# Orders from a scheduler that plays queues and transfers in time, on the bounded path of a two-layer block

## The chip, the cores and the metric

The kernel runs on one core of a Trainium2 chip. Its engines are TensorE (PE, with its weight loads listed apart as PEld), VectorE (DVE), ScalarE (ACT), GpSimd (POOL) and SyncE (SP, which here issues transfers). Each engine works through its own instructions in a fixed order; semaphores hold an instruction back until what it needs from another engine or a transfer is there. The metric is the device time of one launch in microseconds (us). Beside it stands one execution recorded by the hardware profiler; times within it are counted from the start of its span.

## The reference

Two pre-norm layers over 8 sequences of 256 tokens with 256 features, all in fp32. Every block is `x = x + f(layernorm(x))`.

```python
# layer 0, attention: 16 heads of 16; one projection, normed three times
w = x @ W.T;  q, k, v = rms_norm(w, g1), rms_norm(w, g2), rms_norm(w, g3)
att = q @ k.T / 4
y = (softmax(att, -1) + softmax(att, -2)) @ v;   return y @ W
# layer 0, experts: 4 experts, the best 2 of each token, hidden 512, and a shared one of 256
y = sum(combine[:, e] * ((silu(x @ w1[e].T) * (x @ w3[e].T)) @ w2[e].T))
y = y + (silu(x @ sw1.T) * (x @ sw3.T)) @ sw2.T
# layer 1, RWKV-4 time mixing: token shift, three projections, a recurrence over time
xk, xv, xr = (x * tm + shift(x) * (1 - tm) for tm in (tm_k, tm_v, tm_r))
k, v, r = xk @ Wk.T, xv @ Wv.T, sigmoid(xr @ Wr.T)
rwkv = r * layernorm(wkv(decay, first, k, v)) * ln_g + ...;   return rwkv @ Wo.T
# layer 1, experts: 8 experts, the best 2, hidden 256, with biases
h = x @ w1[e].T + b1[e];  y = glu * sigmoid(1.702 * glu) * (lin + 1);  ye = y @ w2[e].T + b2[e]
```

## The kernel before

**Two paths.** A bound on the attention scores is worked out on the device from the gains. With the inputs used it holds, so the first branch of an If is taken: `layers(True)`, the bounded path. It contains everything after the first sequence's norm.

**Units of work.** The sequences form two groups, 0 to 4 and 5 to 7. For each layer and group there is an `Experts` object: `one` and `two` in layer 0 (22 and 15 tiles of 128 gathered tokens are run), `three` and `four` in layer 1 (24 and 16). When all of a group's sequences have their logits (L784), `choose` picks the best two experts of each token, `route` works out which rows go to which tile (L704 to L866, two matmuls at L823 and L824), and `fill` builds the rows' numbers (`here`, `goes`, L885 to L922, matmul L906). Each takes many small DVE operations.

**An expert tile** is: a gather `xg` by POOL (L996); two transposes on PE (L1006) and a copy by ACT (L1008); on PE's sequencer a read of the tile's expert number (`whose`, L1021), by which the weights are addressed; up products (L1014, with w1s and w3s in layer 0, v1s in layer 1); silu on ACT (L1033 or L1028) and a product on DVE (L1035; in layer 1 L1026 and L1029); transposes and a copy again; the down product (L1014, w2s or v2s); out of PSUM by ACT (L1043) or DVE (L1041); a scatter `back` by POOL (L1044). `tiles` overlaps three tiles: it issues the gather of j+3, the transposes of j+1, the up product of j and the down product of j−2 together. After the regular tiles come `spare_tiles`, which read a count (L958) and branch past tiles that are not needed (L962); none of the spare ones runs with these inputs. The shared expert of layer 0 is `shared`: two up products, silu (L944), a product (L945), a down product (L950) and an add to x (L953). `combine` loads the rows back (`y`, L1097 on SP), adds them to x on DVE (L1105, four per sequence), and in layer 1 stores the output (L1109).

**Time mixing** goes through ten stages per sequence. Each step of the generator runs a different stage for each sequence that is under way, so that sequences overlap by a fixed lag:
- norm: statistics (L210, L211) on DVE, a power on POOL (L216, L217), `nb` (L203), `xr` on ACT (L235)
- mix: transposes on PE (L246), a copy on ACT (L1145), `dx` and six `mix` operations on DVE (L1135, L1153)
- project: the matmuls for k, v and r (L1164); k and v are copied by ACT (L1172), r goes through tanh (L1170)
- exponents: scan `pp`, `ex` and `d` on DVE (L1180, L1135); six relus (L1190 to L1192) and two Exps (L1194) on ACT
- denominator, invert, numerator: on DVE a scan `bb` (L1203), `den`, the reciprocal (L1211), a scan `aa` (L1218), `num`
- norm_inner: transposes (L1230) on PE, statistics `st` and `mv` on DVE (L1235, L1236), POOL's power, `z` on ACT (L1241)
- gate, project_out: transposes of z (L246), `num` on ACT (L1251), a product on DVE (L1254), matmuls (L1261), the add to x (L1135)

After them the sequence is normed for the experts (`xm` on ACT, L235), stored for the gathers (L768), transposed (`xmT`), and its logits are computed (L779, L784).

**What sets the order.** The program is written in an order of its own, by `weave`, which draws from several generators in fixed proportions; a tile scheduler then places the instructions on the engines by priority, which is that order but for `tc.high_priority` (an offset of 60 for the stages of time mixing, 3000 for the routing) and `tc.issue_after`, which keeps one instruction behind another. PE's order in the attention part is under `tc.manual_schedule`, that is, as written. The stretch with the most streams is this:

```python
weave((back, 4), (take(mixing, 3), 3), (take(tiles, 5), 5))      # one's combine, two's tiles
weave((take(mixing, 24), 24), (behind(tiles), 13))               # two's tiles
back = two.combine(yp)
...
with tc.issue_after(three.routed.ins):
    weave((shared, 4))                                           # two's last shared products
ctx0.close()                                                     # layer 0's weights end here
...
weave((take(behind(tiles, 3), 20), 20), (mixing, 15))            # three's tiles, sequences 5 to 7
```

`behind(tiles, lag)` keeps each step of the tiles behind a matmul that a sequence has issued. Layer 1's weights (24 transfers by SP, L1308 to L1340) lie where those of layer 0 were, so they wait for the last shared product.

Of the kernel before, what the change touches and what calls it, by code (L numbers as in the profile page):

```python
# [70 lines left out]
def two_layers(  # L71
# [1401 lines left out]
        turned_in = {0: turned(xn, lnp, "xmT1", lambda shape: p0.tile(shape, F32, tag="ps", name="ps"), nc.scalar, bufs=2)}  # L1473
    is_flat = nc.values_load(flat[0:1, 0:1], min_val=0, max_val=1)
    with tc.If(is_flat > 0) as which:
        layers(True)
    with which.Else():
        attention_any()
        layers(False)
# [61 lines left out]
```

## Time and profile before

| | before |
|---|---|
| time, median of 2 runs (759.67 to 761.9) | 760.78 us |
| time of the profiled execution | 762.06 us |
| its span | 760.3 us |
| mean granted TensorE clock | 0.930 |
| busy: PE, DVE, ACT, POOL | 656.0, 462.6, 359.2, 244.9 us |
| moved by DMA | 66.85 MB, 88 GB/s |

By stage, in us from the start of the span, with the busy time of each engine:

| stretch | what runs | PE | DVE | ACT | POOL |
|---|---|---|---|---|---|
| 0–200 | attention, `one`'s logits | 172.2 | 154.8 | 124.3 | 66.4 |
| 200–355 | `one`'s tiles, shared expert | 152.5 | 31.4 | 45.4 | 41.4 |
| 355–530 | `two`'s tiles, sequences 0 to 4 in layer 1 | 152.7 | 119.3 | 99.6 | 45.2 |
| 530–580 | `three`'s routing, last shared products, weights | 32.3 | 44.3 | 17.5 | 10.3 |
| 580–690 | `three`'s tiles, sequences 5 to 7 | 101.6 | 80.1 | 57.6 | 56.8 |
| 690–745 | `four`'s tiles, `three`'s combine | 44.7 | 28.0 | 14.8 | 24.9 |
| 745–760 | `four`'s combine | 0 | 4.8 | 0 | 0 |

The page's parts are read so: busy time per engine; the span in forty slices with a digit of busy tenths each; groups of instructions with what ended the idle time ahead of them. In the lists of waits a row has the waiting engine, tile and line, then what released it, then the total wait, how often, and the longest. In a timeline a row has start and length in us, engine, line, operation, output and input, and in brackets the idle time ahead of it and what ended it.

### The profile page before, as it was taken

The page shows a single profiled execution, that of the slowest core. Times are in us where ns is not written, and L with a number is a line of the kernel's source. Part 1 is how long each engine was busy: PE and PEld are TensorE (multiplying, and loading weights), DVE is VectorE, ACT ScalarE, POOL GpSimd, SP SyncE. Part 2 cuts the span into 40 slices and gives each one's busy share as a digit, 9 for nine tenths or more (in the row PEclk, how much of TensorE's full clock was granted, in tenths as well). Part 3 has the DMA queues.
Part 4 walks back from the last instruction along what each step waited for, and adds up shares of the span by engine and source line. Part 5 has one row for each costly group of instructions (what it writes and reads, how often), then busy time and mean ns, then how long its engine had stood idle before and what let it go on. Part 6 is the DMA issues. An engine that isn't in the chain of part 4 may idle for free. (4 is left out here: it accounts for less than half of the span.)

```text
span 760.3 us, 10764 instructions
## 1 busy us (share of the span) xinstructions
PE 656.0 (86%) x3170; PEld 417.1 (55%) x3170; DVE 462.6 (61%) x1216; ACT 359.2 (47%) x761; POOL 244.9 (32%) x319
## 2 busy tenths in 40 slices
PE   3799999997889999998899888986838989998790
PEld 2355555545775666665466656654625756564460
DVE  6698878787361111110766887673988986755542
ACT  3687767663312333332286477544246474532230
POOL 3434333300202333333222231212040456456440
PEclk9699999988899999999999999998868999999995
DMA  7800000000301111111400110002077336568734
GB/s 205 312 1 15 15 15 15 15 15 18 94 12 31 42 43 49 37 40 52 158 29 13 42 28 22 28 28 71 29 226 257 113 118 190 157 201 259 261 125 137
DMA packets 38547, 66.85 MB, mean 88 GB/s; under 512 B 6006, under 2 KB 20654, under 8 KB 38480
## 3 DMA queue, kind: packets, MB, share of 16 engines
q1 hardware_dynamic: 30400, 47.01, 18.9%
q0 software_dynamic: 7392, 18.50, 7.9%
q8 instruction: 31, 0.51, 0.3%
q10 hardware_dynamic: 688, 0.55, 0.2%
q14 instruction: 36, 0.29, 0.1%
HBM read 51.32 MB, written 16.41 MB: 89 GB/s over the span
## 5 line engine op out<-in xcount | busy, mean ns | idle before, releaser
L996 POOL DMA_INDIRECT xg<-asked,source x77 | 78.5, 1020 | 192.1 <-PE ps L1006 166.3
L1044 POOL DMA_INDIRECT back<-yg,row_i x77 | 81.0, 1051 | 110.6 <-ACT yg L1043 34.4
L1035 DVE TENSOR_TENSOR h<-h,mm 128x512 f32<-128x512 f32 x37 | 25.3, 684 | 108.1 <-PE mm L1014 108.0
L1014 PE MATMUL mm<-v1s,xgT 128*128 x160 | 79.2, 615 | 2.3 <-ACT xgT L1008 1.4
L1008 ACT COPY hT<-ps 128x256 f32<-128x256 f32 (+1 forms) x77 | 36.4, 473 | 94.5 <-PE ps L1006 94.3
L576 ACT ACTIVATE e<-sc,minus 128x512 f32<-128x512 f32 x96 | 59.9, 712 | 31.1 <-PE sc L563 31.0
L1014 PE MATMUL mm<-w1s,xgT 128*128 x148 | 72.8, 611 | 0.2 <-issue 0.2
L1014 PE MATMUL mm<-w2s,hT 128*128 x296 | 72.2, 383 | 0.0
L577 DVE TENSOR_REDUCE s<-e 128x2 f32<-128x512 f32 x96 | 60.5, 677 | 15.9 <-ACT e L576 15.7
L1014 PE MATMUL mm<-w3s,xgT 128*128 x148 | 70.1, 593 | 0.0
L563 PE MATMUL sc<-qT,kT 32*128 32x512 f32 x256 | 58.7, 725 | 2.9 <-DVE qT L544 2.2
L1014 PEld LDWEIGHTS mm<-w2s,hT 128*128 128x128 f32 x296 | 54.0, 192 | 7.2 <-issue 1.4
L515 POOL TENSOR_TENSOR rr<-rr,minus_half 128x32 f32<-128x32 f32 x7 | 38.0, 5429 | 49.8 <-DVE rr L513 49.7
L1006 PEld LDWEIGHTS ps<-ident,h 128*128 128x128 f32 x228 | 29.1, 143 | 44.7 <-issue 28.5
L1164 PE MATMUL sc<-mix,rw 128*128 128x256 f32 x192 | 47.7, 395 | 6.0 <-DVE mix L1153 6.0
L1006 PE MATMUL ps<-ident,h 128*128 128x128 f32 x228 | 39.7, 278 | 8.3 <-DVE h L1029 7.6
L216 POOL TENSOR_TENSOR rs<-mv,eps_ln 128x2 f32<-128x2 f32 x40 | 8.6, 216 | 116.8 <-DVE mv L211 74.4
L1014 PEld LDWEIGHTS mm<-w3s,xgT 128*128 128x128 f32 x148 | 27.6, 191 | 33.3 <-issue 32.6
L1164 PEld LDWEIGHTS sc<-mix,rw 128*128 128x128 f32 x192 | 37.1, 200 | 13.8 <-DVE mix L1153 7.1
L1014 PE MATMUL mm<-v2s,hT 128*128 x160 | 42.7, 386 | 0.8 <-ACT hT L1008 0.8
L1033 ACT ACTIVATE h<-mm 128x512 f32<-128x512 f32 x37 | 22.1, 598 | 42.7 <-PE mm L1014 42.7
L1014 PEld LDWEIGHTS mm<-v1s,xgT 128*128 128x128 f32 x160 | 28.4, 197 | 23.4 <-issue 19.7
(246 smaller groups left out, 1255.9 us busy)
## 6 DMA issues: line engine op xcount, KB each, us to landing
bias<-bd SPq DMA_DIRECT2D x40, 384.0 KB, 4.0
y<-back SPq DMA_DIRECT2D x16, 512.0 KB, 4.7
asked<-xm SPq DMA_DIRECT2D x16, 256.0 KB, 2.2
x<-in_x_dram SPq DMA_DIRECT2D x8, 256.0 KB, 6.1
w1s<-in_w_dram SPq DMA_DIRECT2D x4, 512.0 KB, 9.5
w3s<-in_w_dram SPq DMA_DIRECT2D x4, 512.0 KB, 10.3
w2s<-in_w_dram SPq DMA_DIRECT2D x4, 512.0 KB, 10.2
v1s<-in_v1g_dram SPq DMA_DIRECT2D x8, 256.0 KB, 6.2
```

Of the source, the lines that this page charges most:

```text
L515: on_pool["last"] = nc.gpsimd.tensor_tensor(rr, rr, half, ALU.pow)
L563: nc.tensor.matmul(pa, lhsT=q["kT"][rows, u, ts(t, P)], rhs=q["qT"][rows, u], start=True, stop=True)
L576: nc.scalar.activation(e, pa, AF.Exp, bias=minus)
L577: nc.vector.tensor_reduce(q["s"][:, t, h : h + 2], e, AX.X, ALU.add)
L996: nc.gpsimd.indirect_dma_start(out=xgs[j], out_offset=None, in_=self.asked, in_offset=bass.IndirectOffsetOnAxis(ap=self.source[:, j : j + ...
L1006: nc.tensor.transpose(pt[:, c, :], src[:, ts(c, P)], ident)
L1008: nc.scalar.copy(to, pt)
L1014: nc.tensor.matmul(po.unsqueeze(1), lhsT=lhsT[:, c, :], rhs=w[:, ds(e, 1), c, :], start=(c == 0), stop=(c == n - 1))
L1033: nc.scalar.activation(s, pu, AF.Silu)
L1035: nc.vector.tensor_tensor(s, s, pg, ALU.mult)
L1044: inst = nc.gpsimd.indirect_dma_start(out=self.back, out_offset=bass.IndirectOffsetOnAxis(ap=self.row[:, j : j + 1], axis=0), in_=yg, in_o ...
L1164: last = nc.tensor.matmul(po[:, o, :], lhsT=w[:, c, ts(o, P)], rhs=m[:, c, :], start=(c == 0), stop=(c == NC - 1))
```

## The change

The call of the bounded path is placed in a block whose orders come from another scheduler, one that plays the program in time, with a model of queues and transfers, to choose what each engine gets next. The source of the computation is the same, and so are the written order that it starts from, the priorities, `issue_after` and the hand-written PE order of attention. The other path keeps the plain scheduler.

```diff
     is_flat = nc.values_load(flat[0:1, 0:1], min_val=0, max_val=1)
     with tc.If(is_flat > 0) as which:
-        layers(True)
+        with tc.block(schedule_with_timeline_sim=True):
+            layers(True)
     with which.Else():
         attention_any()
         layers(False)
```

In the compiled program each engine gains one unconditional branch, at the block's start. The other instructions are the same, but for reads of registers and semaphore operations that follow the new neighbours, and for ACT's table loads, of which there are 18 in place of 22 in the block after the first L962. Line numbers after 1475 are one higher.

What moves, by engine, with "#k" for the k-th of its kind:
- PE: attention as before. In the block after the first L962, `z` #k, L1261 #k, the transposes of xr #k+2 and xm #k and L1164 #k+2 stand together, with tile products ahead of them rather than between. Reads of expert numbers (L1021) stand in rows of several: four ahead of the first L950, eight ahead of the L906 of `three`, sixteen ahead of `four`'s first v1s products.
- DVE: `st` #k (L1235) stands behind `bb`, `k`, `den`, `v`, `aa` and `num` of sequence k+1, its `mv`, `nb` and L1254 behind that sequence's reciprocal (L1211). Adds of `combine` (L1105) stand among the operations of `choose`. At the start the conversions of vec and b2s (L1320, L1325) stand ahead of the first `xn`.
- ACT: z, xr, num (L1251) and xm of a sequence stand in a row, behind tile copies that were after them.
- POOL: scatters of `three`'s tiles up to 22 stand ahead of `four`'s first four gathers, which had been ahead of them.
- SP: `combine`'s loads stand earlier, several in a row.

## The prediction

> **What bounds the kernel now.** First I read the page's busy times and its forty slices of 19 us.
>
> ```profile
> PE 656.0 (86%) x3170; PEld 417.1 (55%) x3170; DVE 462.6 (61%) x1216; ACT 359.2 (47%) x761; POOL 244.9 (32%) x319
> ...
> PE   3799999997889999998899888986838989998790
> ...
> DVE  6698878787361111110766887673988986755542
> ```
>
> PE leads at 86%, so the sum of its work sets the end almost everywhere. Two stretches differ: from 360 to 530 us (two's tiles woven with the RWKV sequences 0 to 4) its digits sink to 8, and near 560 to 6, where DVE has 9. Next, what PE waited for from 357 to 530 us (total, times, longest):
>
> ```profile
> PE sc L1261 <- DVE num L1254: 6.1, 3, 2.3
> PE sc L246 <- ACT xm L235: 5.0, 5, 2.0
> PE sc L246 <- ACT xr L235: 3.5, 1, 3.5
> PE ps L1006 <- PEq L962: 2.4, 1, 2.4
> ```
>
> Nearly all are waits for a step of an RWKV sequence. With the rest they come to some 20 us; otherwise expert tiles stand between a sequence's steps in PE's order and cover its latency. Third, DVE's timeline during sequence 2 (start, duration):
>
> ```profile
> 438.30 0.76 DVE L1235 BATCH_NORM_STATS2 st<-sc 128x6 f32<-128x256 f32 x2 [0.32 <-PE sc L1230]
> ...
> 442.60 0.16 DVE L203 SCALAR_TENSOR_TENSOR nb<-mv,rs 128x2 f32<-128x2 f32 x1 [0.79 <-POOL rs L217]
> 442.68 1.27 DVE L1203 TENSOR_TENSOR_SCAN bb<-ex 128x256 f32<-128x256 f32 x2
> ...
> 445.75 0.67 DVE L1254 SCALAR_TENSOR_TENSOR num<-r,num 128x512 f32<-128x512 f32 x1
> ...
> 451.12 3.32 DVE L1211 RECIPROCAL den<-den 128x512 f32<-128x512 f32 x1
> ```
>
> The statistics and gate of sequence 1 (L1235, L1254) run before and among the recurrence of sequence 2 (bb, then the 3.3 us reciprocal). So sequence 1's output and sequence 3's start go on while sequence 2 waits for ACT's exponentials. Last, PE around the change of weights:
>
> ```profile
> 554.43 1.46 PE L950 MATMUL mm<-sw2s,hs 128*128 128x256 f32 x6
> 562.07 0.66 PE L1006 MATMUL ps<-ident,xg 128*128 128x128 f32 x2 [6.19 <-DMA xg<-asked,source]
> ...
> 570.97 7.50 PE L1164 MATMUL sc<-mix,rw 128*128 128x256 f32 x24 [3.88 <-DVE mix L1153]
> ...
> 579.33 1.10 PE L1014 MATMUL mm<-v1s,xgT 128*128 x2
> ```
>
> The weights of layer 1 take the place of layer 0's, so their loads wait for the last shared matmul (ends 555.4); the first v1s matmul comes 23.9 us later.
>
> **The change, part by part.** No arithmetic changes. Every engine gets one branch, and each keeps its instructions in another order. PE's attention order is written by hand and stays. Sums are against the profiled execution (span 760.3, time 762.1, 1.3 above the median of 760.8). "#k" is the k-th sequence.
>
> *Branch.* The page "Runtime: NRT & Kernel Launch" (section "Instruction fetch mechanics") speaks against the change: a taken branch to a target outside the current two pages must fetch it. The rows: far jumps out of the If at the end took 2.8 us (DVE 754.41 to 757.25), branches to nearby targets at L962 0.1 to 0.3 us. The new target follows directly: 0.2, ends 0.1 and 3.
>
> *Start.* On DVE the conversion of vec (its load is issued at 9.9 and lands 4.0 us later) moves ahead of the first xn (13.50), and both L217 powers go behind the second L216 on POOL. DVE waits to about 14, then follows statistics, power and xn: xn near 16.2 in place of 13.5. Some of the 2.7 is absorbed; the first score matmul comes 1.3 later (0 to 2.5).
>
> *One's tiles.* An index read (L1021) takes PE's sequencer 0.69 us to the next (178.48, 179.19, 179.87, 180.55). Four move ahead of the first shared matmul (+1.6); five leave the end of the block, where PE had 2.35 idle (−1.1): +0.5.
>
> *Two's tiles with sequences 0 to 4: the main term.* In the new order PE has z, L1261, the next xr and xm transposes and the next L1164 adjacent, with tiles ahead of the group and none inside. On DVE st#1 (L1235) stands behind bb, k, den, v, aa, h, den and num of sequence 2, so behind the wait for ACT's Exp; its mv, nb and gate L1254 stand behind the 3.3 us reciprocal too. The later sequences are alike. Behind those wait, on PE, L1261#1 and all that follows, so tiles no longer cover. One period, from the first L1164 of k to that of k+1, by the rows of the timelines:
> - k out of PSUM 2.6, pp 1.3, ex and d 1.2: 5.2
> - six relus with v and r on ACT: 9.6; table load 1.28, Exp 1.06: 12
> - bb to num on DVE, with one h: 18.7
> - st with the next st<-x 1.5, reciprocal 3.3, num and mv 0.9: 24.4
> - POOL's two powers, nb: 25.9; z on ACT, its transposes: 27.7
> - num (L1251) 1.0, L1254 0.7, L1261 1.5, with their hand-overs: 32.3
> - x+= and its statistics 1.5, dx 0.7, mix 2.9: 37.2; nb, xm and its transposes: 38.7.
>
> PE's own work in this is two tiles at 6.7 and the sequence's matmuls, about 24; 14 are idle. Before, the periods were 30.2, 25.9 and 25.2 (L1164 at 401.3, 431.5, 457.3, 482.5). In the walk #1 starts at 405.2 (nb#0 behind a combine add delays the first mix), the next period is 33.5, then 38.7, then 39.4 with a tile moved ahead: 438.7, 477.4, 516.8. The last logit of group three follows 48.4 later (46.7 before): 565.2 in place of 529.2, **+36**. If ACT and DVE catch up where I queued them strictly, +10; with a slower matmul clock in the gaps (granted 0.75 from 530 to 580, where PE was idle), +45.
>
> *Route, shared expert, weights.* choose (L704 to L812) is interleaved with a combine add L1105, whose load landed 3.2 after the logit; goes is done 3.8 later. The shared expert's last two tiles stand behind goes, pp#5 and the xr#6 transposes (at 564.9, past the last L950, before). L950 ends about 14.5 after goes, in place of 8.9; with the 3.8 that is some +10 on the start of SP's 24 weight loads and so on the first v1s: **+10.4** (5 to 15).
>
> *Three's first tiles.* L1164#7 and L1261#5 go ahead of tile 0's down product; mix#7 on DVE is ready 13 us after the first v1s: 7 idle, where 2.6 was: +4 (0 to 6).
>
> *Three to four.* On POOL the scatters of tiles up to 22 go ahead of four's first four gathers (issued 672 to 677 before, PE free at 680). A gather takes 1.0 to issue and 3.7 to land, so PE waits 4 to 6. Sixteen index reads stand in a row before four's first v1s: 11.0 us of sequencer. The trace has the sequencer at most 16 matmuls, 4 to 5 us, ahead, which leaves 6. "TensorE: Matmul & The Clock Gate" (specification table) gives PE's queue a depth of 64; with matmul and weight load as two entries that hides 7 and leaves 4. The two waits overlap: **+6** (2 to 9); by the rule it would be +5.
>
> *End.* The index reads leave four's block, but there PE was full already; two L1105 groups go ahead of h and yg: 0 ± 2. The last combine is unchanged.
>
> *ACT.* Table loads fall from 22 to 18, 5.1 us by the row's 1.28. They lie beside PE's work or inside the chain already counted: 0.
>
> **Sum:** 0.2 + 1.3 + 0.5 + 36 + 10.4 + 4 + 6 = 58.4. From 762.1 that is 820.5; less the 1.3 to the median, **819 us**.
>
> **The rivals.**
> - *Faster.* The period is shorter than I walk it: the group of RWKV steps finds its data ready since more tiles stand ahead of it. Then the 3.5 of xr, L1261's 6.1 and the branch's 2.4 go, and nothing comes back: about 749. It decides where a period stays under 25, the two tiles and the sequence's own matmuls. The 17 us of waits speak for it; st behind the reciprocal speaks against it, since no tile ahead of it on PE makes DVE earlier. 4%.
> - *No change that can be told.* PE has 656 us of work by either order, and what idles in one place is regained in the next: 762. For it: PE idles 10 us or more around 560, which could absorb a delay. Against: those waits hang on the same chain and shift with it. Here too the change that does little: attention is fixed by hand. But the block after 357 us is reordered on all five engines. 8%.
> - *Moderately slower.* The main term is only +10, for tiles cover most of the chain; with the other 22: 793, with 783 to 802 its own span. 24%.
> - *As forecast,* 802 to 846: 58%. *Slower still* (each DVE wait also delays scatters and gathers behind it on POOL, or weights come later): 850 and more, 6%.
>
> **How the numbers follow.** The range joins the forecast (its main term between +20 and +45, the small terms at their ends) with the moderate case: 783 to 846; left out are the faster case, the one without change and slower still, 18%. The bound for telling a change is about 2%, 15 us; faster takes 3% (a part of the first rival stays within the bound), within it 9%, slower 88%.
>
> **What would show it.** Right: L1164's starts near 405, 439, 477, 517; PE waiting for L1254 and xm more than 12 us per period in place of 2 to 4; L1235 just before or after the reciprocal; the first v1s near 627; PE's digits at 6 in the slices from 420 to 560; PE's busy time still near 656. Wrong: periods of 30 or less; v1s matmuls before 595; or the loss lying in attention or in four's tiles, where I give 2 and 6.

## The result

| | before | after |
|---|---|---|
| time, median of 2 runs each | 760.78 us (759.67 to 761.9) | 808.05 us (806.26 to 809.84) |
| ratio | | 1.066 (95% interval 1.060 to 1.072) |
| span of the profiled execution | 760.3 us | 808.0 us |
| granted TensorE clock | 0.930 | 0.913 |

The change makes the kernel 47 us slower; forecast were 58. From the page of after, its busy times and two rows of the forty slices (of 20.2 us each):

```profile
PE 667.0 (83%) x3170; PEld 428.8 (53%) x3170; DVE 465.9 (58%) x1216; ACT 352.8 (44%) x757; POOL 246.7 (31%) x319
...
PE   4899999996999999998997676965667799979790
...
DVE  6688787886621111108783636552878885663742
```

PE's share falls from 86% to 83%, and its row shows where: from the 22nd slice to the 30th (424 to 606 us) it has fives, sixes and sevens with a single nine, where before had mostly eights and nines up to 530 us, and DVE's digits there are 2 to 8. Neither engine is full; they wait for each other. PE's busy time rose too, by 11 us, with the same 3170 matmuls.

What PE waited for, in after, from 357 us to the last logit of group three at 561 (total, times, longest):

```profile
PE sc L246 <- ACT xm L235: 12.0, 4, 5.0
PE sc L1261 <- DVE num L1254: 11.5, 4, 6.0
PE sc L246 <- ACT z L1241: 10.5, 4, 4.4
...
PE ps L1006 <- ACTq L962: 0.7, 1, 0.7
```

The first three rows were 5.0, 6.1 and 2.1 us in before's list, whose third row is

```profile
PE sc L246 <- ACT z L1241: 2.1, 4, 0.6
```

Together they grew from 13 to 34 us. The wait at L962 has gone down from 2.4 to 0.7.

The same period of DVE as was shown of before (sequence 2's recurrence, sequence 1's statistics), now in after:

```profile
445.02 1.27 DVE L1203 TENSOR_TENSOR_SCAN bb<-ex 128x256 f32<-128x256 f32 x2 [6.25 <-ACT ex L1194]
...
451.05 0.75 DVE L1235 BATCH_NORM_STATS2 st<-sc 128x6 f32<-128x256 f32 x2
...
452.38 3.33 DVE L1211 RECIPROCAL den<-den 128x512 f32<-128x512 f32 x1
...
459.31 0.16 DVE L203 SCALAR_TENSOR_TENSOR nb<-mv,rs 128x2 f32<-128x2 f32 x1 [0.51 <-POOL rs L217]
461.90 0.69 DVE L1254 SCALAR_TENSOR_TENSOR num<-r,num 128x512 f32<-128x512 f32 x1 [2.43 <-ACT num L1251]
...
468.27 2.46 DVE L1153 SCALAR_TENSOR_TENSOR mix<-dx,vec,x 128x256 f32<-128x256 f32 x6
```

`bb` of sequence 2 starts 12.9 us after that sequence's first L1164 (432.2). The statistics of sequence 1 come behind it and `num`, their aggregation (`mv`) behind the reciprocal. L1254, which had stood at 445.75 in front of the reciprocal, ends at 462.6. PE beside it:

```profile
453.83 1.89 PE L1014 MATMUL mm<-w2s,hT 128*128 x8
459.45 1.36 PE L246 MATMUL sc<-ident,z 128*128 128x128 f32 x4 [3.73 <-ACT z L1241]
462.65 3.42 PE L1261 MATMUL sc<-rw,num 128*128 128x256 f32 x8 [1.84 <-DVE num L1254]
465.90 0.60 PE L246 MATMUL sc<-ident,xr 128*128 128x128 f32 x4
471.49 0.48 PE L246 MATMUL sc<-ident,xm 128*128 128x128 f32 x1 [4.99 <-ACT xm L235]
471.76 5.62 PE L1164 MATMUL sc<-mix,rw 128*128 128x256 f32 x16
```

After the second tile's down product PE has only z, L1261, xr and xm, one behind the other, and is idle 3.73 + 1.84 + 4.99 us between them. The tiles that covered those steps have been done earlier.

A period is the time from the L1164 of one sequence to that of the next. The windows sum the periods up; they begin some 0.3 us ahead of the first L1164 (window, its length, then busy time and instructions of PE, PEld, DVE, ACT, POOL, then PE's granted clock). Before, the whole stretch and the periods of sequences 2 and 3:

```profile
357.00:528.70 171.70, 152.10 (x634) 103.99 (x634) 118.13 (x261) 99.27 (x179) 44.07 (x57) 0.97 0.14 43
...
431.20:457.10 25.90, 23.36 (x106) 16.68 (x104) 19.66 (x43) 16.91 (x31) 7.17 (x10) 0.99 0.10 30
457.10:482.30 25.20, 21.90 (x98) 15.43 (x98) 20.38 (x47) 16.29 (x31) 5.20 (x8) 1.00 0.04 13
```

and after:

```profile
357.00:561.10 204.10, 160.01 (x634) 110.24 (x634) 118.24 (x261) 96.67 (x177) 46.01 (x58) 0.90 0.11 36
...
431.90:471.50 39.60, 27.36 (x101) 18.69 (x101) 21.08 (x47) 17.24 (x32) 7.58 (x10) 0.80 0.07 20
471.50:511.80 40.30, 33.05 (x122) 23.11 (x123) 21.71 (x48) 19.13 (x35) 5.01 (x8) 0.82 0.04 14
```

The same 634 matmuls up to the last logit take 204.1 us in place of 171.7. Of the 32.4, idle time bears 24.5 (19.6 to 44.1) and slower matmuls 7.9 (152.1 to 160.0 busy, clock 0.97 to 0.90).

The table has the shift of after against before at marks of both traces, and what each stretch adds ("tile 3" is the fourth of its group, counted from 0):

| mark | shift, us | added | forecast |
|---|---|---|---|
| first score matmul | +1.6 | +1.6 | +1.3 |
| first transposes of two's tiles | −0.6 | −2.1 | +0.7 (branch, index reads) |
| last logit of group three | +32.4 | +33.0 | +36 |
| first v1s product | +40.7 | +8.3 | +10.4 |
| v1s of three's tile 3 | +48.0 | +7.3 | +4 |
| v1s of three's tile 23, the last | +38.7 | −9.3 | 0 |
| v1s of four's tile 3 | +48.4 | +9.7 | +6 |
| v1s of four's last tile | +46.1 | −2.3 | 0 |
| end | +47.7 | +1.6 | 0 |

### The profile page after: what moved, and what is told of

It is laid out like the page before. It is cut to its first block, busy times and chain, and to the rows that moved or that the text cites. A ratio compares the mean times of both kernels' runs of the same rounds, so it can differ in the third digit from the quotient of the medians.

```text
span 808.0 us, 10830 instructions
## 1 busy us (share of the span) xinstructions
PE 667.0 (83%) x3170; PEld 428.8 (53%) x3170; DVE 465.9 (58%) x1216; ACT 352.8 (44%) x757; POOL 246.7 (31%) x319
## 5 line engine op out<-in xcount | busy, mean ns | idle before, releaser
L996 POOL DMA_INDIRECT xg<-asked,source x77 | 80.2, 1041 | 168.3 <-PE ps L1006 146.1
L1014 PE MATMUL mm<-w2s,hT 128*128 x296 | 70.0, 379 | 0.0
L563 PE MATMUL sc<-qT,kT 32*128 32x512 f32 x256 | 58.4, 693 | 3.1 <-DVE rr L513 2.4
L1164 PE MATMUL sc<-mix,rw 128*128 128x256 f32 x192 | 49.3, 412 | 1.4 <-DVE mix L1153 1.4
L1026 DVE TENSOR_TENSOR hb<-mm,bias 128x512 f32<-128x512 f32 x40 | 27.6, 689 | 34.9 <-PE mm L1014 30.1
L1164 PEld LDWEIGHTS sc<-mix,rw 128*128 128x128 f32 x192 | 39.5, 211 | 9.1 <-issue 2.4
## 6 DMA issues: line engine op xcount, KB each, us to landing
y<-back SPq DMA_DIRECT2D x16, 512.0 KB
w1s<-in_w_dram SPq DMA_DIRECT2D x4, 512.0 KB
w3s<-in_w_dram SPq DMA_DIRECT2D x4, 512.0 KB
w2s<-in_w_dram SPq DMA_DIRECT2D x4, 512.0 KB
```

Source lines behind the costliest of these rows:

```text
L563: nc.tensor.matmul(pa, lhsT=q["kT"][rows, u, ts(t, P)], rhs=q["qT"][rows, u], start=True, stop=True)
L996: nc.gpsimd.indirect_dma_start(out=xgs[j], out_offset=None, in_=self.asked, in_offset=bass.IndirectOffsetOnAxis(ap=self.source[:, j : j + ...
L1014: nc.tensor.matmul(po.unsqueeze(1), lhsT=lhsT[:, c, :], rhs=w[:, ds(e, 1), c, :], start=(c == 0), stop=(c == n - 1))
L1026: nc.vector.tensor_tensor(hb, ph, biases[j][:, 0 : 2 * I2], ALU.add)
L1164: last = nc.tensor.matmul(po[:, o, :], lhsT=w[:, c, ts(o, P)], rhs=m[:, c, :], start=(c == 0), stop=(c == NC - 1))
```

## The experiments

All but one of the experiments use the plain scheduler and the kernel before, with some engines' orders written out. A function adds issue-order edges, without waits, between neighbours of a list of instructions (reads of registers are left where the scheduler puts them):

```diff
+def pin(tc, nc, **orders):
+    ...
+        for a, b in zip(seq, seq[1:]):
+            tc.add_manual_dep(b, a.name, no_sync, reason="pin")
...
+            if is_bounded:
+                pin(tc, nc, PE="...", DVE="...", Activation="...", Pool="...", SP="...")
             three.spare_tiles()
```

Lines of kernel code are 17 higher in those profiles: L1164 is L1181 there, L1241 is L1258, L1254 is L1271. The text goes on with the kernel's own line numbers. The times of before measured beside these runs spread from 750.6 to 765.4 us, so single times decide little; ratios and the periods of the traces do. Ratios are to the kernel before, with a 95% interval.

**Where the loss arises: whole block, first part, second part, other blocks.** The seventh run takes all changed orders between the first L962 and four's spare tiles (`pin` with the after lists). The first takes them only for the instructions that started before 531 us in the kernel before, the eighth only for the later ones:

```diff
# in words: the lists themselves are long
-pin(tc, nc, <after's lists>)                                        # seventh
+pin(tc, nc, <after's order of the early ones> + <before's of the rest>)   # first
+pin(tc, nc, <before's order of the early ones> + <after's of the rest>)   # eighth
```

> All orders of the changed kernel for the block between the first L962 and four's spare tiles (357 to 690 us before), all other orders old, no added branch. By the traces this block carries +49.5 at its end less 1.3 from its start, of which the last block gave 2.3 back: 760.8 + 46 to 48 = 808, ratio 1.062. Rival (the branch, attention and the other blocks bear a fifth or more): 798 or less.

> The plain scheduler, with every engine pinned (by issue-order edges) to the changed kernel's order for the instructions that ran from 357 to 531 us in the kernel before (two's tiles with sequences 0 to 4), and to the old order everywhere else. My theory, that this part bears most of the loss: 793 us (760.8 + 32, the shift of the last logit of group three between the two traces), with L1164 at about 400, 432, 471, 512. Rival, that the loss of this part would be absorbed later by what PE idles near 560, and the rest comes from the route, the weights and the change to four: 775 or less.

> The complement of the first run inside that block: old orders up to 531 us, the changed ones from there (route, shared products, three's tiles, change to four). By the traces: +8 at the last L950, +7 at three's first tiles given back later, +8 to 10 at four's first tiles: 760.8 + 13 to 17 = 775, ratio 1.02. If the two parts add up, first and second give the seventh: 32 + 15 = 47. Rival (the second part costs only because the first upsets it): 765 or less.

Measured: the seventh 1.0636 (1.0573 to 1.0698), 805.7 us; the first 1.0507 (1.0390 to 1.0624), 794.9 us; the eighth 1.0145 (1.0091 to 1.0198), 769.6 us. 5.1% and 1.5% come to 6.5%, beside the 6.4% of both. So the loss lies in the block, some three quarters of it in the stretch of two's tiles with sequences 0 to 4; it is not made up later. In the eighth L1164 keeps near its old pace (395.7, 424.9, 453.4, 478.5: 82.9 us from 1 to 4, before 81.2), and its end is 11.8 us late after correction for a start that was 4.0 early (span 768.1 against 760.3); the forecast of 13 to 17 was a little high.

The twelfth and the eleventh run take the changed orders only in the first block (attention, one's tiles) and only in the last (four's tiles). The tenth has the block and its branch alone:

```diff
-        with tc.block(schedule_with_timeline_sim=True):
+        with tc.block():
             layers(True)
```

> The block with the plain scheduler: all orders as before, one branch more. Prediction's row: 0.2 us, ratio 1.000 with an interval that holds 1. Rival (a taken branch must fetch its target): 3 us, ratio 1.004, hard to tell in the time but seen as 2.5 to 3 us of PE, DVE and ACT at the block's start.

> Old orders but for the first block (attention, one's tiles), which has the changed one. Prediction: 1.3 + 0.5 = 1.8 us, 0 to 3.5, ratio 1.002. By the traces the block's last shared product is 1.1 late and its end, with the index reads moved, 2.3 early: 0.998 to 1.002.

> Old orders but for the last block (four's tiles, three's combine), which has the changed one. Prediction: 0 +- 2. By the traces 2.3 us are given back there after the first tiles: 758 to 761, ratio 0.997 to 1.000.

Measured: the branch alone 1.0012 (0.9988 to 1.0035). PE's first instruction in the block starts at 12.03, in before at 12.04, so a stall like the 2.8 us of the far jump at the end isn't there: the target follows the branch. The rule in the page "Runtime: NRT & Kernel Launch" of the Trainium skill (section "Instruction fetch mechanics") fits this, for it has a fetch only where the target lies outside the two pages held. The first block 1.0043 (1.0021 to 1.0065), 3.3 us, more than the forecast 1.8 and within its bounds; in its one trace the first shared down product (L950) is 1.1 us late and two's tiles are not, so where the rest lies is open. The last block 0.9997 (0.9957 to 1.0038): nothing.

**Which order in the first part.** My forecast named DVE's: the statistics behind the recurrence and the reciprocal. The second run undoes that for sequences 1 and 2, on top of the first run, with POOL's powers; the third undoes the order of PE and ACT instead, by moving the second expert tile of each period behind the next xr; the fourth does both. The edits to the lists are given in words, as moves; k counts sequences.

```diff
 # second: lists of DVE and POOL, k = 1, 2
+move(logit[k-1], st[k], mv[k], st and mv of the next xr, before=bb[k+1]); move(nb's, after=k[k+1])
+move(back of the second tile, after=the powers for those nb's)
 # third: lists of PE, ACT, DVE, POOL
+move(w1s, w3s, h transposes, w2s of the second tile, after=xr[k+2])
+move(h, hT, yg of it, after=num[k]); move(its product, after=mix[k+2]); move(its back, after=powers)
```

> As the first, but for sequences 1 and 2 DVE gets the old place of the inner norm's statistics (logit, st, mv and the next sequence's st and mv ahead of bb of the next sequence, nb right behind k), and POOL's powers for them go ahead of the scatter in front of them. PE's and ACT's orders stay as changed. Theory A (my prediction as written: DVE's order of st behind the recurrence sets the period): some 7 us less for each of two periods, 779. Theory B (the orders are locked together: z on ACT and PE still stands behind the second tile's h, hT and yg, which end near the time at which z came anyway, and the gate stands behind the reciprocal): 0 to 3 a period, 788 to 793.

> As the first, but for sequences 1 and 2 the second tile's products move from ahead of z to behind the next xr's transposes on PE, its h, hT and yg on ACT behind the gate's num, its product on DVE behind mix, its scatter on POOL behind the powers. DVE's statistics stay behind the recurrence. Theory A (DVE's chain sets the period whatever PE does in it): 0 to 1 a period, 791 to 793. Theory C (PE's order, with no tile inside the group, makes the loss): 6 to 7 for each of two periods, 779.

> Both edits, and L1254 of sequences 1 and 2 ahead of the next reciprocal. Theory B (either order alone keeps the chain long, only both together shorten it): periods of 32 in place of 39 to 40, 14 to 16 less in all, 777 to 779. Theories A and C: no more than the better of the two single edits.

Measured: 1.0567 (1.0461 to 1.0674), 1.0692 (1.0607 to 1.0776) and 1.0583 (1.0489 to 1.0676), where the first run has 1.0507. None gains, and the 779 or less that one of the theories gave each of them is missed by 18 us or more. The second shows why DVE's place alone is not enough. Its DVE has the statistics at once (start, duration):

```profile
440.70 0.76 DVE L1252 BATCH_NORM_STATS2 st<-sc 128x6 f32<-128x256 f32 x2 [0.32 <-PE sc L1247]
...
446.16 0.16 DVE L220 SCALAR_TENSOR_TENSOR nb<-mv,rs 128x2 f32<-128x2 f32 x1 [2.02 <-POOL rs L234]
...
449.30 0.66 DVE L1052 TENSOR_TENSOR h<-h,mm 128x512 f32<-128x512 f32 x1
```

but `nb` is followed by z on ACT only here:

```profile
443.58 0.60 ACT L1050 ACTIVATE h<-mm 128x512 f32<-128x512 f32 x1 [1.04 <-PE mm L1031]
451.17 0.58 ACT L1025 COPY hT<-ps 128x512 f32<-128x512 f32 x1 [6.99 <-PE ps L1023]
454.58 0.37 ACT L1060 COPY yg<-mm 128x256 f32<-128x256 f32 x1 [2.83 <-PE mm L1031]
454.85 1.02 ACT L1258 ACTIVATE z<-sc,nb,rs 128x256 f32<-128x256 f32 x2
```

z stands behind hT and yg of the second tile, whose products wait on PE for an h that DVE now gives later (449.30, behind the delayed recurrence: bb starts 17.2 us after L1164, in the first run 13.3). z comes 29.7 us after L1164 of sequence 2 (425.2), later than in the first run (26.1). The fourth did bring z forward, to 21.4 us. But in the third and fourth the moved tile stood ahead of x3, the copy of the next xr, which held back dx by 5.6 us: a fault of the edit. The fifth run mends it in the third, the sixth in the fourth with POOL's powers ahead of the next scatter and gather:

```diff
+move(h, hT, yg of the second tile, after=x3[k+2])                     # fifth and sixth
+move(the powers for nb's, before=the earlier back); move(nb's, after=den[k+1])  # sixth
+move(L1254[k], before=reciprocal[k+1]); move(last two num[k+1], after=mix[k+2])   # sixth
```

> The third run with a fault of its edit mended: there the moved tile's h, hT and yg stood on ACT ahead of the copy of the next xr (x3), which held back dx by 6 us in each of the two periods; now they stand behind that copy. DVE as changed. Theory A (DVE's chain alone sets the period): as the first run, its two periods (L1164 2 to 3 and 3 to 4) 39 to 40, ratio 1.05. Theory C (PE's order makes the loss): periods near 33, ratio 1.03.

> The fifth with DVE's and POOL's orders too: for sequences 1 and 2 statistics ahead of bb, POOL's powers ahead of the scatter and gather that held them back in the fourth run, nb behind the first den, L1254 ahead of the next reciprocal, that sequence's last two num products behind mix. Theory B (orders locked together; only all of them shorten the chain): the two periods 33 to 34 in place of 39 to 40, 11 to 13 us less than the first run, ratio 1.033. Theories A and C: no better than the better single edit.

Measured: 1.0625 (1.0564 to 1.0685) and 1.0478 (1.0428 to 1.0529). Both are short of what was expected: the periods of sequences 2 and 3 are 44.2 and 46.0 us in the fifth, 37.7 and 41.0 in the sixth. The fifth, PE around the group:

```profile
461.27 1.36 PE L263 MATMUL sc<-ident,z 128*128 128x128 f32 x4 [12.28 <-ACT z L1258]
...
478.17 0.33 PE L263 MATMUL sc<-ident,xm 128*128 128x128 f32 x1 [3.66 <-ACT xm L252]
```

z comes 26.5 us after L1164 (434.2), as in the first run, though the tile no longer stands in front of it; PE idles 12.28 us there instead. So with these orders DVE's and POOL's chain sets z, wherever the tile stands on PE, and the tile's work now follows. The longer period is a fault of the edit again. On DVE the last `nb` ahead of xm waited

```profile
477.32 0.16 DVE L220 SCALAR_TENSOR_TENSOR nb<-mv,rs 128x2 f32<-128x2 f32 x1 [4.40 <-POOL rs L234]
```

for a power on POOL behind the moved tile's scatter:

```profile
475.21 1.04 POOL L1061 DMA_INDIRECT back<-yg,row_i  x1 [14.12 <-ACT yg L1060]
```

The sixth has z 19.4 us after L1164 (430.4), 6.7 earlier than the first run:

```profile
449.80 1.02 ACT L1258 ACTIVATE z<-sc,nb,rs 128x256 f32<-128x256 f32 x2 [2.27 <-DVE nb L220]
```

Only the fourth and the sixth, with moves on all four engines, make z earlier. But xm met the same scatter (a wait of 4.13 us), and the period ended at 37.7 us. The ninth run puts the powers for xm ahead of that scatter too and tile 34 (counted from 0 over `one` and `two`), which the new order had moved into the period of 3, back behind L1230 of sequence 3:

```diff
+move(powers for xm[k], before=back of the moved tile)
+move(w1s, w3s, h transposes, w2s, h, hT, yg, back of tile 34, after=L1230[3] and what follows it)
```

> The sixth, where the inner norm came 7.6 us earlier but the expert norm (xm) of the same sequence then waited on POOL behind the moved tile's scatter, and L1164 of 4 behind tile 34. Now POOL's powers for xm stand ahead of those scatters too, and tile 34 stands behind L1230 of sequence 3, as it did before. Theory B (a lock on each of four engines; freed together the chain shortens to what the rows add up to): the two periods 33 each in place of 39.4, logit of the last sequence of group three 13 to 15 us earlier than in the first run, ratio 1.031 to 1.035. Rival (something else than order holds the period, such as the matmul clock in the gaps): periods of 37 or more, ratio 1.045.

Measured: 1.0398 (1.0349 to 1.0446), 790.4 us. The windows of the first run, the whole stretch and then the periods of 2, of 3 and from 4 on:

```profile
357.00:559.90 202.90, 161.31 (x634) 111.70 (x634) 118.10 (x261) 96.75 (x177) 45.13 (x58) 0.89 0.11 36
...
431.10:470.50 39.40, 27.11 (x101) 18.99 (x101) 21.02 (x47) 17.25 (x32) 7.48 (x10) 0.80 0.07 20
470.50:509.80 39.30, 32.80 (x122) 22.77 (x123) 21.66 (x48) 18.68 (x35) 5.00 (x8) 0.84 0.04 14
509.80:559.90 50.10, 37.15 (x156) 27.35 (x154) 21.24 (x47) 22.68 (x41) 9.12 (x13) 0.85 0.06 22
```

and of the ninth:

```profile
357.00:557.80 200.80, 160.49 (x633) 109.90 (x632) 118.59 (x261) 97.06 (x177) 48.88 (x57) 0.89 0.11 36
...
430.80:466.50 35.70, 26.67 (x100) 18.89 (x100) 21.18 (x47) 17.03 (x32) 8.59 (x10) 0.79 0.07 19
466.50:500.80 34.30, 24.88 (x102) 17.77 (x102) 21.20 (x47) 17.71 (x34) 7.93 (x9) 0.85 0.04 16
500.80:557.80 57.00, 43.43 (x174) 30.33 (x174) 22.03 (x48) 24.03 (x44) 9.09 (x14) 0.88 0.06 22
```

The periods fall from 39.4 and 39.3 to 35.7 and 34.3 us, not to 33, and the ratio of 1.0398 lies between the 1.031 to 1.035 of the theory and the 1.045 of the rival. In the period of 2 PE's idle time falls from 12.3 to 9.0. In that of 3 it rises from 6.5 to 9.4; that period is shorter because tile 34 has left it, and the stretch from 4 on has 174 matmuls in place of 156 and takes 6.9 us more. Over the whole stretch idle time goes from 41.6 to 40.3, and the last logit comes 2.1 earlier, not 13 to 15. Part of the rival holds: the clock in the two periods was 0.79 and 0.85, as low as before the edit. The interval of its time overlaps that of the first run, so a gain of the ninth over the first is likely (1.1%) but not settled.

## Why the prediction was right, and where it was off

**The main term** was +36, of which the walk put 3.9 before sequence 1's L1164 and 32 behind it. Measured are −0.7 and 33.1: L1164 at 400.6, 432.2, 471.8, 512.0, where the walk had 405.2, 438.7, 477.4, 516.8. The period that was worked out row by row (38.7, then 39.4) measured 39.6 and 40.3, and its steps are in the trace at their places: bb at +12.9 (walk 12), the reciprocal at +20.2 (20.2), z at +26.7 (25.9), L1254 at +29.8 to 30.4, xm at +38.7. What failed is the term ahead of it: `nb` #0 behind the combine's add delayed nothing that L1164 of sequence 1 still waited for.

Four readings ahead of the result were off, though the sum hardly hangs on them. The order "st behind bb and num" holds for sequences 1 and 2 but not, as the walk and the list of moves have it, for all alike: `st` of 0 and 3 still stands ahead of the next bb (408.3 and 412.8; 519.0 and 522.6), so the long periods are two. Of the signs, PE's waits for L1254 and xm are 6.8 us in each of these two periods and not over 12; with z, which the sign left out, they are 10.6 and 11.2. PE's digit of 6 in before belongs to the slice from 513 to 532 us; near 560 it is 3. And the last L950 of before ends at 555.9, not 555.4.

**What the prediction called the cause** was too narrow in one respect. It named DVE's order, behind which "tiles no longer cover". In the second run the old place of the statistics on DVE and POOL did not bring z forward while ACT and PE kept their order, in the fifth the moves on PE and ACT did not while DVE kept its own; in the fourth and sixth both together did. Shown is the chain and where it lies; which smallest set of moves would give the old pace back isn't: the best edit left PE 40.3 us idle where the first run had 41.6 and before 19.6, while the complete old order in this part (the eighth run) has the old pace.

**Idle or clock.** I counted the loss as idle time and gave the slower clock only to the upper end of the range. By the windows it is 7.9 of the 32.4; the idle time alone is 24.5. The walk came out right because the rows that it took were those of a chain with its waits, in which PE's matmuls have little part: z's transposes and L1261 take 4.8 us of the 39.6 in after, where the same steps of before took 3.0. The two periods measured 0.9 us each above the walk.

**Start and index reads.** DVE waited for vec as walked, until 13.98, and the first score matmul was 1.56 late (forecast 1.3):

```profile
13.98 0.18 DVE L1320 TENSOR_SCALAR vec<-vec 128x16 f32<-128x16 f32 x1 [1.35 <-DMA vec<-in_vecs_dram]
```

At the first L962 I gave the five index reads that move away 1.1 of a gap of 2.35; 1.65 of it went. With a forecast of +2.0 up to there and −0.6 measured, this is 2.6 of the 11 us by which the sum was too high. But the two traces don't compare well here: the granted clock from 0 to 200 us was 0.89 in before and 0.92 in after. Of the traces with the old order in this block, those with a clock near after's begin two's tiles earlier: at 356.7 us with 0.91 (fourth run) and at 355.0 with 0.92 (eighth), where after begins them at 357.2. By this estimate the term is a loss of 0.5 to 2.2 us, and the +3.3 of the twelfth run speaks for a loss too. It is likely and not settled, for the fifth run's trace, with the old order and 0.89, begins them at 360.6.

**Route, shared expert, weights** were +10.4, measured +8.3 in after's trace and about +6.4 in the eighth run's. The steps are there. PE at the change of weights in after:

```profile
594.05 1.89 PE L950 MATMUL mm<-sw2s,hs 128*128 128x256 f32 x8
601.84 0.66 PE L1006 MATMUL ps<-ident,xg 128*128 128x128 f32 x2 [5.90 <-DMA xg<-asked,source]
...
620.03 4.93 PE L1014 MATMUL mm<-v1s,xgT 128*128 x8
```

The transposes of xr #6 stand ahead of the last L950 (at 593.6), which ends 40.0 late, and the first v1s comes 24.1 us after its end, in before 23.4.

**Three's first tiles** were the step that was wrong. I expected 7 us of idle time for mix #7; PE waited 1.38. The +7.3 at tile 3 are L1164 #7 and L1261 #5 (5.4 and 2.0 us), which stand ahead of it now and behind it before; they are given back, and by three's last tile the stretch has gained 2.0 where I had it lose 4. I had priced moved work as lost. With its 6.0 us this is the largest part of the error.

**Three to four** was +6, with a wait of 4 to 6 for the gather and the index reads beside it. POOL in after, with the two scatters ahead of four's first gather:

```profile
720.04 1.10 POOL L1044 DMA_INDIRECT back<-yg,row_i  x1 [2.50 <-DVE yg L1041]
721.48 0.98 POOL L1044 DMA_INDIRECT back<-yg,row_i  x1 [0.34 <-DVE second L917]
722.77 1.00 POOL L996 DMA_INDIRECT xg<-asked,source  x1 [0.30 <-issue]
```

and PE, which waited for it:

```profile
722.07 1.13 PE L1014 MATMUL mm<-v2s,hT 128*128 x4 [1.10 <-ACT hT L1008]
727.48 0.66 PE L1006 MATMUL ps<-ident,xg 128*128 128x128 f32 x2 [4.29 <-DMA xg<-asked,source]
```

The wait was 4.29 us, the whole step +9.7: PE also waited 1.7 for hT and 0.7 for xgT, and the first v1s behind the wait took 3.56 us in place of 1.9. That is a little past the upper bound of 9, but part of it is before's own trace: from three's last tile to four's tile 3 it takes 14.9 us, and the nine other traces that have the old order from there on 17.2 to 18.6, where after takes 24.6. Against those the step is +6 to +7.4, inside the forecast. On to four's last tile before takes 44.2, after 41.9 and those nine 40.6 to 42.9, so that the −2.3 behind the step belongs to the same difference. Of the sixteen index reads fifteen were done at 725 us, within the wait for the gather, and they left no wait of their own. So whether PE's sequencer runs 16 matmuls ahead, as the forecast had it, or has a queue of 64 entries, as the page "TensorE: Matmul & The Clock Gate" of the Trainium skill (specification table) says, made no difference here.

**The rivals.** That tiles moved ahead would let the group find its data ready fell with the first three waits of after's list: more tiles stood ahead of it, and the waits grew from 13 to 34 us. "Regained in the next place" held only for three's tiles, in which work had moved and no time been lost. The moderate case (main term +10) had tiles covering the chain; in after none stands between z and the next L1164.

The sum, then: −2.6 at the start, −3 in the main term, −2 at the weights, −6 at three's tiles, +3.7 at four's, −2.3 and +1.6 after that come to −10.7, which is what the span's 47.7 us lack to the forecast 58.4. The terms at the start and at four's tiles are in part no errors of the forecast but, as said, the particular trace of before.

## What to carry to other kernels

When a kernel is bound by one engine and its orders let long chains of small steps on other engines run beside that engine's bulk work, the order across engines is one object: a new order on one engine is judged by following one period of the chain through every queue it passes, with the durations of a trace. Work that only changes its place in a full queue isn't lost time; what costs is a stretch in which no other work stands between one step of the chain and the next. And a fix for such a stretch has to be followed to the next wait: three times here the named wait went and the next one, for a scatter or a copy in front of the step, took its place.

## What the runs showed of the hardware that was not expected

In the two periods with waits of up to 5.0 us the granted clock of TensorE was 0.80 and 0.82, where the same periods before, with no wait above 2.3, had 0.99 and 1.00. The 634 matmuls of the whole stretch took 5% longer (160.0 us in place of 152.1). The loss in this stretch was thus a third larger than its added idle time (32.4 and 24.5 us).

Runs of the same kernel spread by 2% (before: 750.6 to 765.4 us). In the profiled executions part of this lies in attention: with the same orders there, the granted clock from 0 to 200 us was 0.90 in the ninth run and 0.95 in the second, and sequence 0's first L1164 came at 378.1 and at 372.2 us.
